# Dense tiles of eight heads in layer 0's output, work on the other batch one head pair earlier in attentions 1 and 3, and other PSUM banks in the expert stages

## The chip, the cores and the metric

The kernel runs on one core of a Trainium2 chip. The metric is device time in microseconds, the median over the runs of a kernel. The core has five engines that work beside one another, each on its own queue of instructions: TensorE (PE, with its weight loads as PEld) multiplies matrices and writes to PSUM; VectorE (DVE), ScalarE (ACT) and GpSimd (POOL) do the rest of the arithmetic; SyncE (SP) issues most DMAs. An engine that must wait for another holds up all that stands behind it in its queue. PSUM has eight banks; a bank that TensorE wrote can be written again only when its reader is done.

## The reference

Four layers act on `x` of 4 batches, 256 tokens, 256 features, in float32. Each layer adds a cross-attention to 512 context tokens of 128 features, and then a feed-forward stage. Both get `x` normalised over its features (mean and variance, no weights).

```python
x = x + L0_xattn(LN(x), ctx)        # 16 heads of 16, q and k normalised by head
x = x + L0_ffn(LN(x))               # dense W, and 4 of 64 adapters of rank 16 by norm
x = x + L1_xattn(LN(x), ctx, mask)  # 16 query heads of 128, 8 key/value heads
x = x + L1_ffn(LN(x))               # 2 of 8 experts (176 wide), and a shared one (352)
x = x + L2_xattn(LN(x), ctx, mask)
x = x + L2_ffn(LN(x))               # 1 of 2 experts by token
x = x + L3_xattn(LN(x), ctx, mask)
x = x + L3_ffn(LN(x))               # MLP on the top 12.5% of a batch's tokens
```

Layer 0's attention is the one whose output changes form. Its last 16 context tokens have key and value weights of their own and a softmax of their own:

```python
q = ln(x @ Wq + bq)                      # by head; k and k_dca likewise
ctx = attn(q, k_main, v_main) + attn(q, k_dca, v_dca)
return ctx.reshape(b, s, 16 * 16) @ Wo + bo
```

Layers 1 to 3 are `softmax(q k / sqrt(128)) v` with two query heads to a key head, then `@ Wo`.

## The kernel before, in words

The order of the instructions on TensorE, DVE, ACT and POOL is written out by hand (`manual_schedule`): what stands first in the program stands first in its engine's queue. A float32 matmul is two passes of the array, a transpose by TensorE is one.

**Layer 0.** The loop runs over batch `b`, group of four heads `hg` and half `kp` of the context; `i = 2*hg + kp` is called a half step. A half step issues: scores of this group (L1321, exponential on ACT at L1325, into `pT`); `ahead(b, i)`, which prepares the next batch; `values` of the group before (L1331 for the main context, L1340 for the last 16 tokens); at the second half `quotient`; and `between(b, i)`. The four heads of a group lie on 128 partitions of a bank `po`, 32 rows each: 16 rows that hold the softmax sum (the values have 16 columns of ones ahead of them), and 16 rows of values. `quotient` (L1354 to L1360) transposes 32 x 32 blocks on DVE to get at the sums, takes the reciprocal, transposes back, multiplies, and lets POOL add main and last part to `oT[:, hg]`. So `oT` holds four tiles of 128 partitions of which half the rows are of use. `output0` (L1366) multiplies them, for each of two chunks of 128 tokens, with `wo0`, whose four tiles are Wo's rows laid out to match (four matmuls a chunk); DVE adds the bias (`y_sb`, L1374), POOL adds to `x_sb`. The biases of the values go through the same `wo0`: `bias_columns` (`pbrow`) and `output_bias` (`pbo`, L1281). `output0(b - 1)` comes in half steps 4 and 5 of batch `b`, that of the last batch after the loop.

Keys and queries are normalised by `Scale`: POOL squares (`hs`), DVE sums (`hv`, L1218), ACT forms the roots (`hr`, L1223), DVE multiplies into `pad` (L1231), TensorE transposes (`pT`, L1296). `ahead` spreads this chain over the half steps 2 to 6.

The feed-forward stage of layer 0 works by `Arrows(n)`, one for each of eight chunks: `vectors` (`paf`, L1398), `routes` (DVE, POOL `twof`, L1414 to L1427), `turned` (transposes `puTf`, L1435), `output` (L1444, L1448).

**Attentions 1 to 3.** Query and key weights are multiplied together beforehand, as are value and output weights: `folding` has `pm` (L985, copied by ACT to `m_sb`, L993) and `pn` (L1001, copied by DVE to `n_sb`, L1004), eight pairs of them a layer, in between the work of the stage before. The attention loop has 32 units, `(b, hp)`, hp being one of eight head pairs. In a unit TensorE does the scores (`ps`, L1817), the values (`po`, L1825) and some products for queries or outputs (L1787). The sums of the softmax go over DVE and POOL: halves are added (L1836 on POOL, L1842 and L1844 on DVE), transposed and reduced to `sums` (L1850); after four head pairs TensorE multiplies them with a constant (`pz`, L1857) into the one bank "t", DVE takes the reciprocal (`rz`, L1866), spreads it (`wide`, L1871), and the outputs are multiplied by it (L1872). At the end of the attention, `last_output` (`py`, L1907) needs the last four head pairs of batch 3 divided.

After each unit the attention calls a function, `after(b, hp)`, that works on the batch before: `beside1` in attention 1 (the norm for the feed-forward stage, its transposes, the router `chosen`, L2072 to L2113, almost all DVE), `beside3` in attention 3 (norm, router's weights, `spread`, `places`; and later `gathered`, `rest`, `picked` for the batch before that).

**The banks.** In layer 0 six banks go round ("ring") and two are "o". From the second attention stage on there are four "s", two "mm", one "t" and one "o". The expert stages of layers 1 and 2 run in blocks of gathered tokens: `turn_in` (L2306 in layer 1, L2608 in layer 2) transposes a block into "t", `fall` (`pyr`, L2341, copied out by ACT at L2348) writes to "o". `pn` uses "mm", in turn with `pm`.

Of the kernel before, what the change touches and what calls it, by code (L numbers as in the profile page):

```python
# [17 lines left out]
P = 128  # L18
# [817 lines left out]
def bounded_path(ctx: ExitStack, tc: tile.TileContext, t, out: bass.AP, over):  # L836
# [137 lines left out]
    def folding(L, m_sb, n_sb):  # L974

        for i in range(4):
# [4 lines left out]
            for g in range(2):  # L981
# [18 lines left out]
                pn = bank("mm", [P, 2, D], f"pn_{L}_{i}_{g}")  # L1000
# [25 lines left out]
    with tc.manual_schedule(engines={E.PE, E.Activation, E.DVE, E.Pool}):  # L1026
# [42 lines left out]
        wo0 = l0.tile([P, 4, D], F32, tag="wo0", name="wo0")  # L1069
        nc.sync.dma_start(wo0, t["L0_wo"].rearrange("(g p) n -> p g n", p=P))  # L1070
# [34 lines left out]
        vals = [l0.tile([P, NK, H0, 32], F32, tag=f"vals{i}", name=f"vals{i}") for i in range(2)]  # L1105
        vals_d = [l0.tile([P, H0, 32], F32, tag=f"vals_d{i}", name=f"vals_d{i}") for i in range(2)]

        def ones_of_values():
# [9 lines left out]
            for i in range(2):  # L1118
                nc.gpsimd.memset(vals[i][:, : NK - 1, :, :HD0], 1.0)
                nc.gpsimd.tensor_copy(  # L1120
                    vals[i][:, NK - 1, :, :HD0], rows[:, 0:1, None].to_broadcast([P, H0, HD0])
                )
                nc.gpsimd.tensor_copy(vals_d[i][:, :, :HD0], rows[:, 1:2, None].to_broadcast([P, H0, HD0]))
# [61 lines left out]
        def project_v(b):  # L1185

            wv = by_head(wkv, 2 * HD0)[:, :, :, HD0:]
            for k0 in range(0, NK + 1, 2):
                pv = bank("mm", [P, 2, H0, HD0], f"pv{b}_{k0}")
                for k in range(k0, min(k0 + 2, NK + 1)):  # L1190
                    ck = c_last[:, b % 2, k - NK + 1, :] if k >= NK - 1 else cT[:, b, k * P : (k + 1) * P]
                    nc.tensor.matmul(pv[:, k - k0], lhsT=ck, rhs=wv[:, int(k == NK)], start=True, stop=True)
                if k0 < NK:
                    nc.scalar.copy(vals[b % 2][:, k0 : k0 + 2, :, HD0:], pv)
                else:
                    nc.scalar.copy(vals_d[b % 2][:, :, HD0:], pv[:, 0])
# [67 lines left out]
        bcol = l0.tile([P, 4, P], F32, tag="bcol", name="bcol")  # L1264

        def bias_rows():

            nc.vector.tensor_tensor(brow[:, 0, :], brow[:, 0, :], brow[:, 1, :], ALU.add)

        def bias_columns():  # L1270
            pc = bank("o", [P, 4], "pbrow")
            for g in range(4):
                nc.tensor.matmul(
                    pc[:, g : g + 1], lhsT=brow[:, 0, g * P : (g + 1) * P], rhs=ident[:1, :1], start=True, stop=True
                )
            nc.vector.tensor_copy(bcol, pc[:, :, None].to_broadcast([P, 4, P]))

        def output_bias():
            pb = bank("mm", [P, D], "pbo")
            for g in range(4):  # L1280
                nc.tensor.matmul(pb, lhsT=bcol[:, g, :], rhs=wo0[:, g, :], start=(g == 0), stop=(g == 3))  # L1281
# [45 lines left out]
        def values(b, hg, pT, po, ks, dca):  # L1327

            for k in ks:
                for j in range(4):  # L1330
                    nc.tensor.matmul(  # L1331
                        po[32 * j : 32 * (j + 1), 0, :],
                        lhsT=vals[b % 2][:, k, 4 * hg + j, :],
# [4 lines left out]
            if dca:  # L1338
                for j in range(4):
                    nc.tensor.matmul(  # L1340
                        po[32 * j : 32 * (j + 1), 1, :],
                        lhsT=vals_d[b % 2][:, 4 * hg + j, :],
# [5 lines left out]
        def quotient(b, hg, po, oT):  # L1348
# [6 lines left out]
            rz = small.tile([P, NB0], F32, tag="rz0", name=f"rz0_{b}_{hg}")  # L1355
            nc.vector.reciprocal(rz, z[:, :, 0])
            nc.vector.transpose(z, rz[:, :, None].to_broadcast([P, NB0, 32]))
            o = w0.tile([P, 2, S], F32, tag="o0", name=f"o0_{b}_{hg}")
            nc.vector.tensor_tensor(o.rearrange("p a s -> p (a s)"), po, z_f, ALU.mult)
            nc.gpsimd.tensor_tensor(oT[:, hg, :], o[:, 0], o[:, 1], ALU.add)  # L1360

        def output0(b, chunks=range(NC)):
            for c in chunks:
                py = bank("mm", [P, D], f"py0_{b}_{c}")
                for hg in range(4):
                    nc.tensor.matmul(  # L1366
                        py,
                        lhsT=oTs[b][:, hg, c * P : (c + 1) * P],
                        rhs=wo0[:, hg, :],
                        start=(hg == 0),  # L1370
                        stop=(hg == 3),
# [89 lines left out]
        xnTs[0] = layernorm_T(xn, "a0_0")  # L1461
        centred(by_head(wq0), by_head(wq0), mq)
# [51 lines left out]
        def between(b, i):  # L1514
# [25 lines left out]
            if b > 0 and i in (4, 5):  # L1540
                output0(b - 1, (i - 4,))
# [1654 lines left out]
```

## Time and profile before

| what | value |
|---|---|
| median of 3 runs | 1453.56 us (1453.41, 1453.56, 1455.87) |
| the profiled execution | 1455.58 us |
| its span | 1453.9 us |
| mean granted TensorE clock | 0.994 |
| TensorE busy | 1421.4 us |
| DVE, POOL, ACT busy | 914.0, 677.1, 585.9 us |
| layer 0's attention, feed-forward | about 20 to 146 us, 146 to 240 us |
| attentions 1, 2, 3 | about 240 to 569 us, 705 to 1000 us, 1090 to 1415 us |

The span is from the first to the last instruction of the profiled execution, and the time around it is part of the execution's own time. Busy time says how much of the span an engine worked; a row of a group gives its total busy time, the mean duration of one instruction, and the idle time ahead of it with what ended that. Matmuls overlap in the array, so that their durations are longer than the distance from one start to the next. The granted clock is given as a share of full speed: at 0.50 a matmul takes twice as long.

### The profile page before, as it was taken

What the parts mean: (1) busy time and instruction counts of PE and PEld (TensorE: products, weight loads), DVE (VectorE), ACT (ScalarE), POOL (GpSimd) and SP (SyncE); (2) the same over time, 40 slices, a digit from 0 to 9 for tenths busy, and PEclk for the clock granted to TensorE, in tenths of its full rate; (3) what the DMA queues carried; (4) which work ended last, traced back from release to release, by engine and by line L of the source; (5) the groups of instructions that cost most, each with busy time, mean ns of one, the idle gap of its engine ahead of it and who ended that gap; (6) DMA issues with size and microseconds to landing.
All of it is one profiled execution on the core that took longest, in us unless ns stands there. A gap on an engine that the chain in (4) does not pass through costs nothing.

```text
span 1453.9 us, 20222 instructions
## 1 busy us (share of the span) xinstructions
PE 1421.4 (98%) x7421; PEld 937.0 (64%) x7421; DVE 914.0 (63%) x2004; ACT 585.9 (40%) x1124; POOL 677.1 (47%) x796
## 2 busy tenths in 40 slices
PE   9999999999999999999999999999999999999998
PEld 7665676566556666777556666655875566666656
DVE  6666773666676556543576666548755766767675
ACT  4666343433433332244543333333454433333331
POOL 2222232576655454131366665665314765456560
PEclk9999999999999999999999999999999999999999
DMA  5000220310000001164020000000331000000000
GB/s 167 2 2 2 73 72 1 79 32 0 8 1 8 1 8 32 39 203 103 30 72 2 23 1 1 8 0 8 95 124 44 19 1 1 0 1 0 0 1 32
DMA packets 49591, 47.06 MB, mean 32 GB/s; under 512 B 8169, under 2 KB 45386, under 8 KB 49484
## 3 DMA queue, kind: packets, MB, share of 16 engines
q1 hardware_dynamic: 45884, 37.56, 8.6%
q0 software_dynamic: 2496, 6.82, 1.8%
q8 instruction: 61, 1.00, 0.3%
q10 hardware_dynamic: 1104, 1.31, 0.3%
q14 instruction: 46, 0.38, 0.1%
HBM read 38.86 MB, written 6.82 MB: 31 GB/s over the span
## 4 chain that ended last, share of the span: by engine, by line
PE 88%; DVE 7%; POOL 2%; issue 1%; ACT 1%; DVEq 0%; ACTq 0%; POOLq 0%
PE ps L1817 22%; PE po L1825 21%; PE paq L1787 5%; PE pao L1787 4%; PE pbq L1787 4%; PE pbo L1787 4%; PE pgu L2325 2%; PE ps L1321 2%; PE pyf L1448 2%; PE po L1331 2%; PE paf L1398 1%; PE py L1907 1%; PE pm L985 1%; PE psh L2161 1%; PE pn L1001 1%
## 5 line engine op out<-in xcount | busy, mean ns | idle before, releaser
L1836 POOL TENSOR_TENSOR half<-pT 128x1024 f32<-128x1024 f32 x93 | 218.8, 2353 | 322.6 <-ACT pT L1820 255.2
L1817 PE MATMUL ps<-qT,cT 128*128 128x512 f32 x768 | 345.5, 592 | 0.0
L1825 PE MATMUL po<-pT,c_sb 128*128 128x512 f32 x768 | 345.3, 592 | 0.0
L1820 ACT ACTIVATE pT<-ps,mbias 128x512 f32<-128x512 f32 x384 | 263.7, 687 | 155.5 <-PE ps L1817 143.9
L1825 PEld LDWEIGHTS po<-pT,c_sb 128*128 128x128 f32 x768 | 145.8, 190 | 183.2 <-issue 183.2
L1817 PEld LDWEIGHTS ps<-qT,cT 128*128 128x128 f32 x768 | 138.9, 190 | 138.4 <-issue 137.0
L1829 ACT COPY oT<-po 128x512 f32<-128x512 f32 x96 | 56.2, 586 | 265.0 <-PE po L1825 265.0
L1872 POOL TENSOR_TENSOR oT<-oT,wide 128x512 f32<-128x512 f32 x90 | 115.5, 1304 | 27.9 <-DVE wide L1871 27.9
L1325 ACT ACTIVATE pT<-ps 128x512 f32<-128x512 f32 x128 | 66.1, 603 | 37.8 <-PE ps L1321 37.6
L1797 DVE TENSOR_TENSOR qT<-qT,paq 128x128 f32<-128x128 f32 x90 | 25.5, 283 | 85.8 <-ACT qT L1796 85.7
L1797 DVE TENSOR_TENSOR w<-w,pao 128x128 f32<-128x128 f32 x21 | 6.0, 285 | 109.4 <-ACT w L1796 109.4
L1844 DVE TENSOR_TENSOR half<-half 128x512 f32<-128x512 f32 x96 | 71.0, 740 | 2.5 <-POOL half L1836 2.2
L1846 DVE STREAM_TRANSPOSE turned<-half 128x512 f32<-128x512 f32 x96 | 68.3, 712 | 6.3
L1787 PEld LDWEIGHTS paq<-xnT_a,m_sb 128*128 128x128 f32 x360 | 57.9, 191 | 21.5 <-issue 10.6
L1787 PE MATMUL paq<-xnT_a,m_sb 128*128 128x128 f32 x360 | 71.4, 280 | 0.1
L1787 PE MATMUL paq<-xx,m_x 128*128 128x128 f32 x360 | 69.8, 276 | 0.0
L1850 DVE TENSOR_REDUCE sums<-turned 128x16 f32<-128x512 f32 x96 | 65.9, 686 | 3.4
L1787 PE MATMUL pao<-n_x,ox 128*128 128x128 f32 x336 | 65.4, 276 | 0.3 <-POOL ox L1713 0.3
L1871 DVE STREAM_TRANSPOSE wide<-rz 128x512 f32<-128x512 f32 x96 | 62.2, 686 | 0.1
L1796 ACT COPY qT<-paq 128x128 f32<-128x128 f32 x90 | 23.9, 265 | 89.9 <-PE paq L1787 89.8
L1800 DVE TENSOR_TENSOR qT<-qT,pbq 128x384 f32<-128x384 f32 x90 | 49.9, 554 | 9.4
L1787 PEld LDWEIGHTS paq<-xx,m_x 128*128 128x128 f32 x360 | 54.6, 192 | 0.0
(445 smaller groups left out, 2612.9 us busy)
## 6 DMA issues: line engine op xcount, KB each, us to landing
wo<-in_L_wo SPq DMA_DIRECT2D x12, 512.0 KB
wq<-in_L_wqT SPq DMA_DIRECT2D x11, 512.0 KB
yd<-yr SPq DMA_DIRECT2D x23, 128.0 KB
w<-in_F_w SPq DMA_DIRECT2D x4, 512.0 KB
xd<-xn_f SPq DMA_DIRECT2D x7, 256.0 KB
wk<-in_L_wkT SPq DMA_DIRECT2D x11, 128.0 KB
wv<-in_L_wvT SPq DMA_DIRECT2D x11, 128.0 KB
x_sb<-in_x SPq DMA_DIRECT2D x4, 256.0 KB
```

Of the source, the lines that this page charges most:

```text
L1325: nc.scalar.activation(pT[kp][:, j], ps[j], AF.Exp)
L1787: nc.tensor.matmul(p[:, at, :], lhsT=lhsT, rhs=rhs, start=(k == 0 and at == 0), stop=(k == len(of) - 1 and i == which[-1]),)
L1817: nc.tensor.matmul(ps, lhsT=cT[:, b, k * P : (k + 1) * P], rhs=qT, start=True, stop=True)
L1820: nc.scalar.activation(pT[:, k, :], ps, AF.Exp, bias=mbias[:, b, k : k + 1])
L1825: nc.tensor.matmul(po, lhsT=c_sb[:, b, k, :], rhs=pT[:, k], start=(k == 0), stop=(k == NK - 1))
L1829: done["head"] = nc.scalar.copy(raw, po).ins
L1836: nc.gpsimd.tensor_tensor(half, pT[:, 0:2], pT[:, 2:4], ALU.add)
L1844: nc.vector.tensor_tensor(part, half[:, 0], half[:, 1], ALU.add)
L1846: nc.vector.transpose(turned.rearrange("p f i -> p (f i)"), part)
L1850: nc.vector.tensor_reduce(sums[b, hp // 4][:, hp % 4, :], turned, AX.X, ALU.add)
L1871: nc.vector.transpose(wide, rzs[b, hp // 4][:, hp % 4, :, None].to_broadcast([P, NB, 32]))
L1872: eng.tensor_tensor(outs[b, hp], outs[b, hp], wide.rearrange("p f i -> p (f i)"), ALU.mult)
```

## The change

There are four groups of edits.

1. Layer 0's output. Groups `hg` 0 and 1 share one tile of `oT`, and 2 and 3 the other: even groups have their values in rows 16 to 31 of each 32 and odd ones in rows 0 to 15. `vals` and `vals_d` are laid out accordingly, so the value weights are copied once into the new order by POOL (`wvo`), the values' copies by ACT go in two halves, and the ones are filled in halves. `quotient` writes the reciprocal into one of two columns of a persistent, zeroed `rz0`, so that the rows of the other group are multiplied by zero, and POOL adds an odd group's two parts to what the even group left. `wo0` has two tiles, read by eight DMAs of 16 partitions. `output0`, `pbrow` and `pbo` use two matmuls in place of four. `output0(b - 1)` comes in half steps 6 and 7 in place of 4 and 5, for batches 1 and 2 (in the last batch it stays at 4 and 5). After the loop, `arrows[0].turned()` and `output()` come ahead of the last batch's output.
2. `beside1`: everything one head pair earlier (hp 3 to 6 in place of 4 to 7).
3. `beside3`: the same, and `gathered`, `rest` one head pair later (hp 1 and 2 in place of 0 and 1), `picked` with `rest`.
4. Banks: `turn_in` of both expert stages takes "t" and "o" in turn, `fall` takes "mm", and `pn`, once the ring is gone, takes "o".

```diff
-                pn = bank("mm", [P, 2, D], f"pn_{L}_{i}_{g}")
+                pn = bank("mm" if "ring" in banks else "o", [P, 2, D], f"pn_{L}_{i}_{g}")
...
-        wo0 = l0.tile([P, 4, D], F32, tag="wo0", name="wo0")
-        nc.sync.dma_start(wo0, t["L0_wo"].rearrange("(g p) n -> p g n", p=P))
+        wo0 = l0.tile([P, 2, D], F32, tag="wo0", name="wo0")
+        wo0r = t["L0_wo"].rearrange("(q o j i x) n -> o j i x q n", q=2, o=2, j=4, i=2)
+        for o in range(2):
+            for j in range(4):
+                r0 = 32 * j + HD0 * (1 - o)
+                nc.sync.dma_start(wo0[r0 : r0 + HD0], wo0r[o, j, 1])
...
+        halves = [(slice(HD0, 32), slice(0, HD0)), (slice(0, HD0), slice(HD0, 32))]
+
+        rz0 = [l0.tile([P, 2 * S // 32, 2], F32, tag=f"rzh{i}", name=f"rzh{i}") for i in range(2)]
+        wvo = l0.tile([P, 2, 2, H0 // 2, HD0], F32, tag="wvo", name="wvo")
...
-                if k0 < NK:
-                    nc.scalar.copy(vals[b % 2][:, k0 : k0 + 2, :, HD0:], pv)
-                else:
-                    nc.scalar.copy(vals_d[b % 2][:, :, HD0:], pv[:, 0])
+                for o, (h, _) in enumerate(halves):
+                    if k0 < NK:
+                        nc.scalar.copy(vals[b % 2][:, k0 : k0 + 2, o, :, h], pv[:, :, o])
+                    else:
+                        nc.scalar.copy(vals_d[b % 2][:, o, :, h], pv[:, 0, o])
...
             pb = bank("mm", [P, D], "pbo")
-            for g in range(4):
-                nc.tensor.matmul(pb, lhsT=bcol[:, g, :], rhs=wo0[:, g, :], start=(g == 0), stop=(g == 3))
+            for g in range(2):
+                nc.tensor.matmul(pb, lhsT=bcol[:, g, :], rhs=wo0[:, g, :], start=(g == 0), stop=(g == 1))
...
-            rz = small.tile([P, NB0], F32, tag="rz0", name=f"rz0_{b}_{hg}")
-            nc.vector.reciprocal(rz, z[:, :, 0])
-            nc.vector.transpose(z, rz[:, :, None].to_broadcast([P, NB0, 32]))
+            odd = hg % 2
+            rz = rz0[odd]
+            nc.vector.reciprocal(rz[:, :, 1 - odd], z[:, :, HD0 * odd])
+            nc.vector.transpose(
+                z.rearrange("p f (i x) -> p f i x", i=2), rz[:, :, :, None].to_broadcast([P, NB0, 2, HD0])
+            )
             o = w0.tile([P, 2, S], F32, tag="o0", name=f"o0_{b}_{hg}")
             nc.vector.tensor_tensor(o.rearrange("p a s -> p (a s)"), po, z_f, ALU.mult)
-            nc.gpsimd.tensor_tensor(oT[:, hg, :], o[:, 0], o[:, 1], ALU.add)
+
+            oT = oT[:, hg // 2, :]
+            nc.gpsimd.tensor_tensor(oT, oT if odd else o[:, 1], o[:, 0], ALU.add)
+            if odd:
+                nc.gpsimd.tensor_tensor(oT, oT, o[:, 1], ALU.add)
...
-                for hg in range(4):
+                for q in range(2):
                     nc.tensor.matmul(
                         py,
-                        lhsT=oTs[b][:, hg, c * P : (c + 1) * P],
-                        rhs=wo0[:, hg, :],
-                        start=(hg == 0),
-                        stop=(hg == 3),
+                        lhsT=oTs[b][:, q, c * P : (c + 1) * P],
+                        rhs=wo0[:, q, :],
+                        start=(q == 0),
+                        stop=(q == 1),
                     )
...
+        for n in range(2):
+            wv = by_head(wkv, 2 * HD0)[:, n, :, HD0:].rearrange("p (q o j) x -> p o q j x", q=2, o=2)
+            for o in range(2):
+                nc.gpsimd.tensor_copy(wvo[:, n, o].rearrange("p (q j) x -> p q j x", q=2), wv[:, o])
...
-            if b > 0 and i in (4, 5):
-                output0(b - 1, (i - 4,))
+
+            i0 = 4 if b == B - 1 else 6
+            if b > 0 and i in (i0, i0 + 1):
+                output0(b - 1, (i - i0,))
...
         arrows[1].routes()
+        arrows[0].turned()
+        arrows[0].output()
         output0(B - 1)
...
-            arrows[n].turned()
+            if n:
+                arrows[n].turned()
...
-                arrows[n].output()
+                if n:
+                    arrows[n].output()
...
-            if hp == 4:
+            if hp == 3:
                 ahead1[b] = Norm(b - 1, f"f1_{b - 1}")
+            elif hp == 4:
+                ahead1[b] = ahead1[b].tokens()
             elif hp == 5:
-                ahead1[b] = ahead1[b].tokens()
+                turned1(b - 1, ahead1[b])
             elif hp == 6:
-                turned1(b - 1, ahead1[b])
-            elif hp == 7:
                 chosen(b - 1)
...
-                    pt = bank("t", [P, ND, P], f"pxg{self.j}")
+                    pt = bank("to"[self.j % 2], [P, ND, P], f"pxg{self.j}")
...
-                    py = bank("o", [P, D], f"pyr{j}")
+                    py = bank("mm", [P, D], f"pyr{j}")
...
-            pt = bank("t", [P, ND, P], f"pxg2_{self.j}")
+            pt = bank("to"[self.j % 2], [P, ND, P], f"pxg2_{self.j}")
...
-            if hp == 4:
+            if hp == 3:
                 routers[b - 1] = Router(b - 1)
-            elif hp == 5:
+            elif hp == 4:
                 routers[b - 1].tokens()
                 routers[b - 1].weights()
+            elif hp == 5:
+                routers[b - 1].spread()
             elif hp == 6:
-                routers[b - 1].spread()
-            elif hp == 7:
                 routers[b - 1].places()
         if b > 1:
-            if hp == 0:
+            if hp == 1:
                 routers[b - 2].gathered()
-            elif hp == 1:
+            elif hp == 2:
                 routers[b - 2].rest()
-            elif hp == 2 and b == 3:
-                picked(0)
+                if b == 3:
+                    picked(0)
```

## The prediction

> **What bounds the kernel now.** I read the page first, then the table of stretches, then TensorE's waits, then single stretches.
>
> ```profile
> span 1453.9 us, 20222 instructions
> ...
> PE 1421.4 (98%) x7421; PEld 937.0 (64%) x7421; DVE 914.0 (63%) x2004; ACT 585.9 (40%) x1124; POOL 677.1 (47%) x796
> ...
> PE 88%; DVE 7%; POOL 2%; issue 1%; ACT 1%; DVEq 0%; ACTq 0%; POOLq 0%
> ```
>
> TensorE works 1421.4 of 1453.9 us and carries 88% of the chain of waits. Only two things can help: fewer passes of the array, or a part of the 32.5 us in which it idles. Where these lie, the stretches show (columns: time, its length, busy time of PE, PEld, DVE, ACT, POOL, granted clock, DMA share, GB/s):
>
> ```profile
> 20.00:146.00 126.00, 120.51 (x1345) 78.72 (x1344) 82.75 (x166) 81.72 (x158) 30.34 (x42) 1.00 0.04 11
> 146.00:240.00 94.00, 90.48 (x463) 64.47 (x462) 63.30 (x116) 39.16 (x90) 29.41 (x27) 1.00 0.18 57
> 240.00:557.00 317.00, 315.45 (x1351) 191.83 (x1351) 194.34 (x418) 122.57 (x211) 181.49 (x216) 1.00 0.06 16
> 557.00:705.00 148.00, 140.58 (x807) 111.19 (x806) 71.94 (x220) 54.55 (x155) 36.14 (x41) 0.97 0.33 96
> 705.00:1000.00 295.00, 293.81 (x1249) 178.86 (x1248) 182.01 (x403) 111.05 (x188) 172.27 (x196) 0.99 0.05 16
> 1000.00:1100.00 100.00, 96.92 (x522) 75.57 (x521) 67.38 (x150) 46.72 (x95) 35.90 (x41) 1.00 0.26 80
> 1100.00:1408.00 308.00, 307.03 (x1325) 186.86 (x1324) 212.72 (x431) 114.56 (x194) 178.49 (x204) 1.00 0.03 8
> 1408.00:1454.00 46.00, 38.11 (x266) 32.87 (x264) 26.91 (x74) 7.97 (x19) 7.42 (x11) 0.95 0.07 25
> ```
>
> The bodies of attentions 1 to 3 (rows 3, 5, 7) leave 1.6, 1.2 and 1.0 us: nothing is to be had inside them. Layer 0 leaves 5.5 us, its FFN 3.5, the stretch behind attention 1 leaves 7.4. TensorE's waits name the places:
>
> ```profile
> PE pz L1857 <- DVE sums L1850: 3.4, 3, 2.6
> PE pxg L2608 <- ACT xnT_f L940: 1.7, 1, 1.7
> PE py L1366 <- POOL oT L1360: 1.6, 1, 1.6
> PE pT L1296 <- DVE y_sb L1374: 1.4, 1, 1.4
> PE pysh L2178 <- ACT m_sb L993: 0.6, 1, 0.6
> PE pxg L2961 <- DVE rz L1866: 0.6, 2, 0.3
> ```
>
> **Layer 0.** Removed: in the output 2 of 4 matmuls for each of 8 chunks.
>
> ```profile
> L1366 PE MATMUL py<-wo,oT 128*128 128x256 f32 x64 | 15.8, 390 | 1.6 <-POOL oT L1360 1.6
> ```
>
> 64 records are 32 matmuls of two passes. A pass of 256 columns takes 0.215 us from start to start in undisturbed rows (0.39 in the row is latency), so 32 passes are 6.9 us; 4 passes of pbo are 0.9 more, and 2 of 4 one-column pbrow matmuls 0.3. So 8.1 us of TensorE is taken out, 1.72 for each batch's output. It comes through only where the array is the bound. By batch:
> - Batch 0: only pbo and pbrow shrink. TensorE waits twice here for the chain DVE sums, ACT square root, DVE pad (1.4 us at 47.2, 1.0 at 51.5), which does not shorten. The copies of the values to their halves, 3 on ACT (512 wide 0.58, 256 wide 0.38), become 6, about 0.25 us more, ahead of that chain's ACT part. I put the start at 0.
> - Batch 1: output0(0) leaves half steps 4 and 5 for 6 and 7. Then py no longer covers the pad chain: hv 71.73 to 73.72 on DVE, hr on ACT till 75.25 (behind four exponentials), pad product at 77.27 to 79.03. The transposes pT at 81.00 would now start about 3.4 us of PE work earlier, and wait for that chain, which gains about 0.5. In return the 1.42 us wait of pT at 83.07 for y_sb (the copy out of a bank, queued on DVE behind the next Norm) goes, and the outputs come back later at half price. I count 1.72 + 1.58 less about 1.4 of new waits for pad and y_sb: 1.9.
> - Batch 2: the same without the 1.58: 1.72 less a wait for pad of about 0.6: 1.1.
> - Batch 3: its outputs stay at 4 and 5, 1.7. A wait of 1.3 at 130.4 (pxn behind a quotient on DVE) stays.
> - The start of the FFN: TensorE waited 1.75 from start to start (1.6 in the row) for POOL's oT at 163.30, because POOL was busy with twof from 160.21 to 162.14. Now the set that needs twof (turned(0), output(0)) stands ahead of py. It must wait for 162.14, about 1.9 in the same place; the wait of py lies behind it. Gain 1.72 + 1.75 - 1.9 = 1.6. arrows[0] leaves its later place; DVE's routes(2) comes about 1.2 us later, and is needed at 182: free.
>
> Added at nothing: POOL's four wvo copies (a 128x256 copy is 0.42 in its rows) at 8 to 10 us, before the values need them; twelve smaller fills for six, about 0.8 us more, ending some 3 us before the first use at 32.6; the second add (0.74) of each odd head group, 8 in all, on a POOL that is busy 30 of 126 us. Only the last of these is near the path, and it is inside the 1.9.
>
> wo0 is read by 8 DMAs of 16 partitions, 32 KB each, in place of one of 512 KB. Rows: SP took 0.43 us to issue wo at 10.13, so seven more add 3 us, ahead of bo, wa, wb, ww and the bias; wo itself and bo are first used at 40.5 and 44, the others from 146 on. The Trainium skill speaks against this: "DMA: Bandwidth & Descriptors", Rules for kernel authors, wants many small transfers coalesced, since under 64 KB one pays mostly overhead. By the trace's issue row it is 3 us on SP hidden by 25 us; by the rule, with eight overheads laid one behind the other at the roughly 2 us that the page gives as fixed cost of its GpSimd path, an estimate of 16 us from 10, still before 40. I take 0. Sum for layer 0: **6.3** (bounds 3.5, if the chains of batches 1 and 2 eat all, and 9).
>
> **Attention 1, work moved up one head pair.** At hp 4 to 7 an undisturbed head pair lasts 8.43 us, all TensorE. The sums on DVE are ready 3.2 us before pz needs them at hp 3; with the Norm there, slack falls to 1.2 to 1.85, as in attention 2, whose Norm is at hp 3 already. No wait, so 0 in the body. At the end chosen(2) sits on DVE (558.61 to 561.87) ahead of the last sums:
>
> ```profile
> 562.00:565.60 3.60, 0.96 (x9) 0.80 (x8) 2.80 (x6) 0.27 (x1) 0.00 (x0) 1.00 0.01 2
> 565.60:569.00 3.40, 3.40 (x18) 3.40 (x17) 3.33 (x5) 0.00 (x0) 1.27 (x1) 0.50 0.00 0
> ```
>
> pz starts at 564.88, 2.8 us late. Without chosen the sums are there at about 560.9, and pz starts at 562.07. Behind it pbo takes 2.7 us, now at full clock, then py must wait for the division chain (rz, wide on DVE, oT on POOL: pz + 4.0 for its first tile, + 5.9 for its last): a new wait of 1.2. py starts at 566.1 in place of 569.49: 3.4, less 0.2 for its last tile: **3.2** (bounds 1.4, the chain being longer than read; 4.5, wait and half clock both gone).
>
> The clock: in this trace the array was busy 0.96 of 3.6 us, and the next 3.4 us ran at 0.50, at a price of 1.7. A stall of 1.75 at 163.30 left it at 1.00. The Trainium skill, "TensorE: Matmul & The Clock Gate", The HAM clock gate, gives half rate after an idle window of about 3.4 us, in windows that run free. By its word a partly busy window costs nothing; by the row it costs 1.7. The row decides; the 1.2 that is left is nearer the 1.75 that cost none. Half clock also stands at 599.8 to 606.6 and 777.3 to 780.7. As everything before them moves by about 9 us, windows may fall otherwise: 1.7 each way on each.
>
> **Banks in the expert stages.** Block loop of layer 1: 2.76 us a block, TensorE bound, nothing; its last fall waits 0.7 for yr (one bank): 0.7. Second turn_in at 613: pgu waits for DVE's we at 614.3 anyway: 0. pysh at 684.3, behind an ACT copy: 0.8. Layer 2: second turn_in 0.6; pxg of block 5 at 1048.7, bank held by xnT_f: 1.8. Against it, pn gets one bank, and each pn must await the copy of the one before:
>
> ```profile
> 696.22 1.12 PE L1001 MATMUL pn<-wo,wv 128*128 128x512 f32 x2 [0.69 <-ACT m_sb L993]
> 696.38 0.80 DVE L925 TENSOR_SCALAR xn_a<-x_sb,mv_a,rstd_a 128x256 f32<-128x256 f32 x2 [0.84 <-POOL rstd_a L920]
> 697.10 1.28 DVE L1004 COPY n_sb<-pn 128x512 f32<-128x512 f32 x2
> ```
>
> The copy lasts 0.69 and the pm between two pn 0.9, so mostly it is free. Here DVE is held by the Norm's wait for POOL: two copies end at 697.8 and 698.4, so the pn of 696.22 waits till 697.8, 1.6, of which about 0.6 is the wait of the pm behind it: -1.0. The same in layer 3's fold (1086.32 against a copy that ends at 1087.43): -1.1. Sum 0.7 + 0.8 + 0.6 + 1.8 - 2.1 = **1.8** (bounds -1 and 4).
>
> **Attention 3.** pxg waits behind pz's bank for rz twice, 0.53 from start to start at 1260.9 and 1344.6; a head pair later rz is not in the way: 1.1. The last pz, 0.64 late behind places: 0.5. Sum **1.6** (0.5 to 1.7).
>
> Sum 6.3 + 3.2 + 1.8 + 1.6 = 12.9. The profiled execution lasted 1455.58 (1.7 outside its span), 2.0 above the median of 1453.56; its span would go to 1441.0. From the median: **1440.7**.
>
> **Rivals.**
> 1. Layer 0 isn't TensorE's any more: with py at half price the pad chain sets batches 1 and 2, and the FFN start waits for twof as long as before for oT. For it: DVE 82.8 and ACT 81.7 of 126 us, and the waits at 47 and 51. Layer 0 then gives 3.5 and pn's bank takes 1 us more: 12.9 - 2.8 - 1 = 9.1, so 1444.5, and with a half-clock window more 1446.2. Chance 0.22.
> 2. More comes: attention 1's tail gives 4.5, layer 0 7.5, and one half-clock window falls away: 1.3 + 1.2 + 1.7 more, 1436.5. For it: the waits exist, and the windows hang on phase. Chance 0.14.
> 3. Slower: pn's single bank. If DVE stands 1.3 us late at each of the 14 follow-on folds of layers 2 and 3, as at 696, that is 14 x 1.3 = 18 us against 2.1 counted: 1456.6. It decides from a copy that ends more than 0.2 us after the pm between. Against it: in the other twelve follow-on folds the trace has the copy end before the next pn starts, though five times only by 0.05 to 0.1. Chance 0.04.
> 4. The change does not do what it says: moved Norms push pz late where they land, so that waits only change place and gain stays under 2.9: slack 1.2 speaks against it. Chance 0.03, 1452.
>
> Mine: 0.57. The range of 8 in 10 takes my case with clock windows of 1.7 each way and most of 1 and 2: 1435.5 to 1446.5. About 0.2% (2.9 us) is what a measurement can tell from no change here: faster 0.93, same 0.03, slower 0.04.
>
> **What would show it.** Right: 32 records of L1366's matmul; the pz wait of 2.6 gone, and one of about 1.2 at the last py; the L2608 and pysh waits gone; new waits of pn for n_sb near 690 and 1080; new waits of pT for pad in layer 0. Wrong: layer 0 shorter by under 4 or over 8 us, waits of pz in hp 4 of attentions 1 or 3, or half clock in other windows than before.

## The result, and the profile after

The changed kernel takes 1443.36 us (median; 1440.92 to 1444.77), the kernel before 1453.63 in the same comparison: ratio 0.9924, interval 0.9907 to 0.9941, a gain of 8.6 to 13.5 us where 12.9 was forecast. A second comparison gave 0.9923 (0.9909 to 0.9937). The spans of the two profiled executions differ by 10.9 us.

The page and the stretches of the changed kernel come first. The stretches are cut at the same work as those shown of before (columns as there).

```profile
span 1443.0 us, 20195 instructions
...
PE 1413.3 (98%) x7381; PEld 931.5 (65%) x7381; DVE 895.7 (62%) x2005; ACT 585.8 (41%) x1136; POOL 684.1 (47%) x816
```

```profile
20.00:143.80 123.80, 118.23 (x1310) 75.17 (x1309) 80.60 (x163) 81.18 (x166) 35.48 (x56) 0.97 0.05 15
143.80:236.40 92.60, 88.91 (x455) 63.02 (x455) 64.23 (x120) 39.04 (x90) 30.88 (x30) 1.00 0.18 57
236.40:553.40 317.00, 315.45 (x1357) 192.52 (x1356) 191.65 (x437) 122.76 (x212) 180.70 (x217) 1.00 0.06 16
553.40:698.80 145.40, 139.63 (x801) 111.08 (x800) 71.08 (x202) 54.37 (x154) 36.09 (x40) 0.96 0.34 98
698.80:992.20 293.40, 292.05 (x1249) 177.37 (x1248) 181.88 (x403) 111.05 (x188) 172.36 (x196) 1.00 0.05 16
992.20:1091.50 99.30, 96.70 (x522) 76.36 (x521) 67.58 (x150) 46.52 (x95) 35.96 (x41) 1.00 0.26 80
1091.50:1397.80 306.30, 306.05 (x1330) 187.12 (x1329) 199.32 (x434) 114.39 (x194) 178.88 (x206) 1.00 0.03 8
1397.80:1443.00 45.20, 37.79 (x261) 32.33 (x259) 25.76 (x71) 8.22 (x20) 7.06 (x10) 0.98 0.07 26
```

Lengths against before: layer 0's attention 126 to 123.8, its feed-forward stage 94 to 92.6, attention 1 the same to 557, then 148 to 145.4, attention 2 295 to 293.4, layer 2's stage 100 to 99.3, attention 3 308 to 306.3, the end 46 to 45.2. Two things stand out. Layer 0's clock fell from 1.00 to 0.97, and attention 2, which nothing in the change touches, is 1.6 shorter, with a clock of 1.00 for 0.99.

TensorE's waits:

```profile
PE pn L1001 <- DVE n_sb L1004: 4.4, 3, 2.3
PE puTf L1461 <- POOL twof L1453: 3.0, 2, 1.8
PE pT L1315 <- DVE pad L1244: 2.7, 3, 1.5
...
PE py L1943 <- POOL oT L1908: 0.9, 3, 0.5
...
PE pz L1893 <- DVE sums L1886: 0.3, 1, 0.3
```

The old waits (pz 2.6, pxg of layer 2, pysh, py for oT, pT for y_sb, pxg for rz) are gone. New are the waits of pn for the copy of the pn before, of pT for pad, and most of puTf's for twof (3.0 in two waits, where before had one of 1.3). The output's matmuls are half as many:

```profile
L1392 PE MATMUL py<-wo,oT 128*128 128x256 f32 x32 | 8.7, 399 | 0.0
```

Matching the starts of the same work in both profiles gives each part's share. "Profile" is how much earlier the work behind the part starts than in the profile of before, less what was gained ahead of it.

| part | forecast | profile | part alone or undone, by ratio of runs |
|---|---|---|---|
| layer 0 with its feed-forward stage | 6.3 | 3.65 | 7.1 (5.2 to 9.2) alone |
| tail of attention 1 | 3.2 | 3.2 | 3.6 (2.5 to 4.8) alone |
| turn_in, fall, and pysh | 3.9 | 3.9 | 2.6 (1.5 to 3.6) alone, pysh not in it |
| pn on one bank | -2.1 | -3.9 | about -3.1, undone, with pysh's wait back |
| attention 2 (clock) | 0 | 1.6 | |
| attention 3 | 1.6 | 2.6 | 3.2 (1.7 to 4.5) alone |

The profile's column adds up to 11.0 before rounding. In layer 0's row 0.6 is no gain: the first scores start that much earlier in this span than in before's, and in other spans up to 0.9 later. The runs' column adds up to 13.4, with intervals of a microsecond or two on each row, because an execution may hold one 1.7 us clock window more or less than the next.

### The profile page after: what moved, and what is told of

It reads as the page before. It is cut to its first block, busy times and chain, and to the rows that moved or that the text cites. A ratio compares the mean times of both kernels' runs of the same rounds, so it can differ in the third digit from the quotient of the medians.

```text
span 1443.0 us, 20195 instructions
## 1 busy us (share of the span) xinstructions
PE 1413.3 (98%) x7381; PEld 931.5 (65%) x7381; DVE 895.7 (62%) x2005; ACT 585.8 (41%) x1136; POOL 684.1 (47%) x816
## 5 line engine op out<-in xcount | busy, mean ns | idle before, releaser
L1836 DVE TENSOR_TENSOR qT<-qT,pbq 128x384 f32<-128x384 f32 x90 | 49.9, 554 | 10.1 <-PE ps L1853 0.9
```

## The experiments

Gains in microseconds are worked out from the ratio and the kernel before of the same comparison (1455.3, 1455.3 and 1455.0 us).

### The changed kernel again

No edit.

> The changed kernel once more, for a second profile and more runs. In its first profile layer 0 up to the end of its feed-forward stage was 3.65 us shorter than before (forecast 6.3), and the clock was at 0.50 from 28.3 to 31.7 and from 48.8 to 52.2. Theory 1: those windows are chance of phase, as the array idles 1.5 us there before as after; this profile has them elsewhere or not at all, and without them layer 0 is 6 to 7 us shorter than before. Theory 2: the change brings them (a wait of 1.8 for pad at 47.9 in place of 1.45), so they stand there again and layer 0 gains 3.6 again. Both: median 1442 to 1444.

Measured: 1444.88, ratio 0.9923 (0.9909 to 0.9937). The granted clock in the first profile of the changed kernel, with the window ahead of each slow one:

```profile
24.90:28.30 3.40, 2.97 (x31) 1.86 (x27) 1.75 (x6) 2.89 (x6) 3.40 (x15) 1.00 0.07 16
28.30:31.70 3.40, 3.40 (x9) 2.22 (x8) 0.00 (x0) 1.62 (x4) 0.48 (x3) 0.50 0.00 0
45.30:48.70 3.40, 1.92 (x23) 1.55 (x23) 3.23 (x7) 3.01 (x7) 0.00 (x0) 1.00 0.00 0
48.70:52.10 3.40, 3.40 (x27) 1.80 (x29) 3.26 (x8) 1.41 (x2) 1.64 (x3) 0.51 0.00 0
```

And the second profile of the same kernel:

```profile
28.90:32.30 3.40, 3.40 (x13) 2.33 (x14) 0.52 (x1) 1.34 (x3) 0.22 (x1) 0.50 0.00 0
48.70:52.10 3.40, 3.07 (x42) 1.89 (x39) 3.22 (x9) 1.87 (x3) 1.45 (x2) 1.00 0.00 0
131.30:134.70 3.40, 3.40 (x32) 1.50 (x32) 0.37 (x1) 2.06 (x4) 0.68 (x1) 0.50 0.00 0
```

The window at 28 stands again, the one at 49 does not, and one at 131 has come. So a window is not bound to the code: which waits are followed by half clock differs between executions of one kernel. Theory 1's stronger half did not show: layer 0 was again two windows poorer, and only 2.4 shorter than before (counted from the first scores, 2.1 here and 3.1 in the first profile).

### pn on its two banks

```diff
-                pn = bank("mm" if "ring" in banks else "o", [P, 2, D], f"pn_{L}_{i}_{g}")
+                pn = bank("mm", [P, 2, D], f"pn_{L}_{i}_{g}")
```

> The changed kernel with pn back in the two banks mm. Theory 1: pn's single bank costs a wait and a half-clock window at the Norm of each fold: the waits of 2.5 at 689 and 2.0 at 1077 go back to the 1.5 and 0.85 of before, the stretch from the last turn_in of layer 1 to attention 2 is 2.5 shorter, the fold before attention 3 1.5 shorter: together 3 to 4 us below the changed kernel, 1439.5 to 1440.5. Theory 2: the Norm's own wait on DVE for POOL sets when attention starts, and the bank only shows it: under 1 us, 1442.5 to 1443.4.

Measured: 1441.74, ratio 0.9901 (0.9886 to 0.9916), against 0.9923 with pn on "o" on the same chip: 3.1 us better, as theory 1 has it and three times what theory 2 allows, though the two intervals overlap a little. What the single bank does is read in the changed kernel, PE first and then DVE (start, duration, instruction, idle before):

```profile
689.11 1.13 PE L1001 MATMUL pn<-wo,wv 128*128 128x512 f32 x2 [2.30 <-DVE n_sb L1004]
```

```profile
687.65 0.80 DVE L925 TENSOR_SCALAR xn_a<-x_sb,mv_a,rstd_a 128x256 f32<-128x256 f32 x2 [0.85 <-POOL rstd_a L920]
688.37 0.68 DVE L1004 COPY n_sb<-pn 128x512 f32<-128x512 f32 x1
```

The copy is queued on DVE behind the Norm, the Norm waits 0.85 for POOL, and pn starts when the copy ends at 689.05. That is the wait that was forecast (2.47 from start to start in place of 0.86 and 0.65: -1.0). What was not in the sum came behind it:

```profile
687.10:690.50 3.40, 1.40 (x6) 0.92 (x7) 1.63 (x4) 1.25 (x5) 2.60 (x4) 0.99 0.14 39
690.50:693.90 3.40, 3.40 (x12) 2.26 (x11) 0.99 (x2) 1.51 (x5) 1.77 (x2) 0.50 0.39 116
```

TensorE stood 2.0 of 3.4 us, and the next 3.4 us ran at half clock, in both profiles of the changed kernel (690.5 and 691.1). With pn on "mm" there is no half clock between 601 and 1436.

But the wait does not always bring the window. Three kernels further down (`fill0` under "Work in layer 0's waits", `dense_out45` under "The outputs at half steps 4 and 5", `arrows_later` under "The first adapters behind the last output") also have pn on "o", with the same wait of 2.2 to 2.3 at this fold, and none has half clock behind it. `fill0`:

```profile
686.80:690.20 3.40, 1.57 (x8) 1.09 (x9) 1.80 (x4) 1.07 (x5) 2.60 (x4) 1.00 0.13 39
690.20:693.60 3.40, 3.40 (x20) 2.41 (x20) 0.97 (x2) 2.58 (x7) 1.60 (x2) 1.00 0.40 116
```

By matched starts this fold costs 0.9 in these three profiles and 2.4 to 2.5 in the two with the window. The second one, at 1077, costs 1.4 to 1.7 in four profiles, and 2.5 in `fill0`, where half clock follows at 1075.9. So the single bank costs 2.3 to 2.6 by itself, and 1.0 to 1.5 more in an execution that has one of these windows. Putting pn back also brings back a wait of pysh (further down), so that the 3.1 of the runs is what is left after that.

### Layer 0 alone

The kernel before with all edits to layer 0 and no other.

> The kernel before with the layer 0 edits alone (dense tiles, outputs in half steps 6 and 7, arrows[0] first). Forecast was a gain of 6.3. Theory 1 (half-clock windows of chance hid part of it): 5 to 6.5 us below before, 1447 to 1448.6, and in the profile no new wait of more than 1 us except the one for pad at 48. Theory 2 (the pad chain and the start eat it): 3 to 4 us below, 1449.6 to 1450.6.

Measured: 1448.28, ratio 0.9951 (0.9937 to 0.9964): 7.1 us. Theory 2's 3 to 4 is outside, theory 1's 5 to 6.5 inside. Its profiled execution was the slowest of its runs (1449.75 of 1447.52 to 1449.75) and has half clock at 28.3 and at 48.8; its layer 0 looks, like the changed kernel's first, only 3.6 shorter.

Nor is the kernel before free of windows in layer 0. The profile of the kernel that has its layer 0 unchanged, and attention 1's edit alone, shows them behind the wait of 1.3 for xn:

```profile
130.40:133.80 3.40, 2.34 (x32) 1.44 (x36) 2.60 (x8) 1.88 (x4) 1.45 (x2) 1.00 0.01 2
133.80:137.20 3.40, 3.40 (x36) 1.83 (x28) 1.37 (x3) 1.73 (x4) 0.08 (x1) 0.50 0.00 0
137.20:140.60 3.40, 3.40 (x27) 1.49 (x20) 2.06 (x4) 2.07 (x4) 0.74 (x1) 0.50 0.02 5
```

All three profiles with the old layer 0 besides that of before have them there. That one had none, and carried a window at 777 instead. Counted from the first scores to the feed-forward stage's second set of chunks, the old layer 0 takes 1.6, 3.2 and 3.2 us longer in those three than in the profile of before. The five profiles with the new layer 0 and nothing else in it (the changed kernel twice, this one, `pn_mm` with pn on its two banks, and `pn_first_o` below) take 2.1 to 4.9 less than it, 3.6 in the mean. The two means lie 5.6 apart. So one pair of profiles undersells this part, and 5.6 is inside the runs' interval, below the 6.3 that was forecast.

### Work in layer 0's waits

```diff
                 pt = bank("t", [P, 4, P], f"pT{b}_{c}")
+                for _ in range(6 if (b, c) == (1, 0) else 0):
+                    nc.tensor.matmul(pt[:, 0, :], lhsT=ident, rhs=ident, start=True, stop=True)
...
         pt = bank("t", [P, ND, S], f"pxn_{name}")
+        for _ in range(2 if name == "a0_1" else 0):
+            nc.tensor.matmul(pt[:, 0, :P], lhsT=ident, rhs=ident, start=True, stop=True)
```

> The changed kernel with eight extra 128x128 matmuls on TensorE: two ahead of the transposes of batch 1's norm (a wait of 0.4 at 26.0), six ahead of the first transposes of batch 1's pad (a wait of 1.8 at 47.9); they write banks that the transposes then overwrite, and stand in waits. Theory 1 (the array's idleness in these waits brings the half-clock windows at 28.3 and 48.8): no half clock from 24 to 56, 1.5 to 3 us below the changed kernel, 1440.4 to 1442. Theory 2 (windows come from elsewhere, or don't come in most runs): within 0.7 us of the changed kernel.

Measured: 1443.25, ratio 0.9916 (0.9903 to 0.993), against 1444.88 and 0.9923: better by 1.0 (ratio) or 1.6 (medians), inside the noise of both. The profile is clear:

```profile
24.00:56.00 32.00, 30.81 (x344) 21.15 (x346) 22.12 (x51) 21.14 (x40) 10.36 (x23) 1.00 0.05 14
```

Full clock through batch 0, and none of the windows of layer 0 was slow. That is no accident of one profile: all seven profiles with the new layer 0 and no extra products have a half-clock window between 28 and 53 us, and the three with them (this one, `best` and `best_plist` below) have none. In this profile layer 0's parts can be read without the clock: from the first scores (24.5 in before) to the feed-forward stage's second set it is 5.1 shorter than before, batch 0 at 0.0 (forecast 0).

### The outputs at half steps 4 and 5

```diff
-            i0 = 4 if b == B - 1 else 6
-            if b > 0 and i in (i0, i0 + 1):
-                output0(b - 1, (i - i0,))
+            if b > 0 and i in (4, 5):
+                output0(b - 1, (i - 4,))
```

> The changed kernel with output0(b-1) in half steps 4 and 5 for every batch, as before; the tiles stay dense. In the changed kernel's profiles batches 1 and 2 gained 1.3 and 1.2 us, where the output's passes alone are 1.7 each: the rest went into new waits for pad (0.9 twice), and for qT and y_sb. Theory 1: at 4 and 5 the output covers the pad chain again, the waits for pad go, and each batch gains its 1.7, so 0.5 to 1 us below the changed kernel: 1442.4 to 1444.4 on the chip of the last runs (where it had 1444.9). Theory 2: the move was what the saving needed, since pT waits for y_sb behind the Norm on DVE (1.6 at 83 before): 1 to 2.5 us above the changed kernel.

Measured: 1446.97, ratio 0.9945 (0.9932 to 0.9959): 3.2 us above the changed kernel by ratio, 2.1 by median. Theory 2. The wait that was 1.4 in before:

```profile
PE pT L1315 <- DVE y_sb L1400: 3.6, 2, 2.3
```

With the output's passes halved and left in place, TensorE reaches pT earlier and waits 2.3 in batch 1 and about 1.3 in batch 2 (no such wait in before) for a copy (y_sb) that sits on DVE behind the Norm. Half clock follows from 84.4 to 91.2. So half of the 1.7 that is taken out of batch 1 at 4 and 5, and three quarters of batch 2's, is waited for at once: batch 2, which the half clock does not reach, gains 0.6 in place of the changed kernel's 1.2. Moving the outputs behind the pad chain costs waits of 0.9 for pad, and takes these away. How the 2.1 to 3.2 us divide between the waits and the half clock was not measured, and the interval overlaps that of the changed kernel a little.

### The first adapters behind the last output

The two edits that move `arrows[0].turned()` and `output()` are undone.

> The changed kernel with arrows[0].turned() and output() back in their place behind the last output. Theory 1: the last py then waits for POOL's oT, now two adds of 0.74 behind twof, about 2.5 us; of the 1.4 that the start of the feed-forward stage gained only 0.1 is left: 1.0 to 1.5 us above the changed kernel. Theory 2: the wait for twof took the place of the wait for oT, one for one, and the order is worth nothing: within 0.4.

Measured: 1446.14, ratio 0.9935 (0.9921 to 0.9949): 1.3 (median) to 1.7 us above the changed kernel. The intervals overlap, but the profiles settle it for theory 1: the start of the feed-forward stage gains 1.4 over before in the changed kernel and 0.0 here. The wait, against 1.8 for twof in the changed kernel:

```profile
PE py L1392 <- POOL oT L1386: 3.3, 1, 3.3
```

POOL makes twof first, and then the two adds of an odd group. In the changed order the wait for twof covers them, and the last py waits for nothing.

### Attention 3 alone

> The kernel before with the edits to beside3 alone. Forecast 1.6; in the two profiles of the changed kernel the stretch from 1170 to 1421 is 2.5 shorter. Theory 1: 2.5, of which 1.1 are the waits behind pz's bank, 0.6 the last pz, and the rest weight loads or copies that no longer stand beside the scores' products, in every run. Theory 2: 1.6, and the remaining 0.9 comes with another edit (the phase of other parts): 1.4 to 1.8 us below before.

Measured: 1452.07, ratio 0.9978 (0.9969 to 0.9988): 3.2 us, theory 1; 1.4 to 1.8 is at the interval's edge. The part that the forecast lacked shows in before, not among TensorE's waits but among those of its weight loads:

```profile
PEld paq L1787 <- DVE xnT_a L1721: 0.2, 1, 0.2
```

At 1236.5 and 1320.5 the query products start 0.42 late in all (start to start), as DVE is late with the folded input of the next queries. One head pair later this DVE work meets other neighbours, and most of the 0.42 is gone, twice. 2 x (0.53 + 0.42) + 0.6 is 2.5; the part is 2.6 shorter in this kernel's own profile as in the changed kernel's.

### turn_in and fall alone

> The kernel before with turn_in on t and o in turn, and fall on mm; pn stays in mm. Forecast 3.9 for these (0.7, 0.8, 0.6, 1.8). Theory 1: these waits are all on the path: 3.5 to 4.3 us below before, nothing new behind them. Theory 2: what is gained in the blocks is waited for again at the gathers of the Norm behind them (POOL): under 2.5 us.

Measured: 1452.60, ratio 0.9982 (0.9975 to 0.999): 2.6 us, between the two theories. The waits of 0.6 and 1.8 in layer 2 and 0.7 at the last fall are gone, 3.1 in all, of which matched starts show 2.7 as gained (2.0 and 0.6 before rounding); but the one of pysh, 0.8 in my sum, stays:

```profile
PE pysh L2178 <- ACT m_sb L993: 0.6, 1, 0.6
```

So that 0.8 was put to the wrong edit. It is pn that frees it (the same wait is there in `pn_mm`, and not in the changed kernel, whose work behind it gains 1.1): pysh takes an "mm" bank that a fold's first pm holds until ACT's copy, and finds the other one free if pn is elsewhere.

### Attention 1 alone

> The kernel before with the edits to beside1 alone. Forecast 3.2, and in both profiles of the changed kernel the stretch from 558 to 576 is 3.3 shorter. Theory 1: 2.8 to 3.8 us below before, pz no longer waits, and py waits about 0.4 and 0.7 for the divided outputs. Theory 2 (the shift only trades one clock window for another, as those behind plist at 600): under 1.5.

Measured: 1451.75, ratio 0.9975 (0.9967 to 0.9983): 3.6 us, theory 1. The window that holds the end of attention 1 in the changed kernel, to be set against 0.96 of 3.6 busy and then 0.50 before:

```profile
558.90:562.30 3.40, 3.14 (x27) 2.90 (x26) 3.30 (x6) 0.00 (x0) 1.27 (x1) 1.00 0.00 0
```

The tail is 3.2 shorter by matched starts in this kernel's own profile too. In the changed kernel pz no longer waits; py waits 0.43 and 0.68 from start to start for the divided outputs, 1.1 in all, where 1.2 was forecast.

### pn on "o" for a layer's first two folds, and more work in waits

```diff
-                pn = bank("mm" if "ring" in banks else "o", [P, 2, D], f"pn_{L}_{i}_{g}")
+                pn = bank("o" if i == 0 and "ring" not in banks else "mm", [P, 2, D], f"pn_{L}_{i}_{g}")
```

> The changed kernel with pn on o only for the first two of each layer's eight folds, and on mm for the rest. In the profile of banks_turn_fall (pn on mm throughout) the wait of pysh of 0.8 behind the ACT copy of pm stays; in the changed kernel it is gone. Theory 1: that 0.8 belongs to pn, since pn on o leaves pysh the other mm bank; here both are had: 0.5 to 1 us below pn_mm, 3.6 to 4.2 below the changed kernel. Theory 2: the wait moves to the next pm or pn: equal to pn_mm within 0.4.

Measured: 1440.08, ratio 0.9901 (0.9886 to 0.9916): 3.2 us better than the changed kernel, and the same ratio as pn_mm, as theory 2 has it. But the wait of pysh is gone from the profile and comes nowhere else: by matched starts the work behind it gains 1.1 here and 0.1 in pn_mm. So theory 1's mechanism holds, and its size is below what these runs can tell.

`best` adds to it the extra matmuls of above, and five ahead of batch 3's first feed-forward transposes; `best_plist` adds also:

```diff
+                    if n == 0:
+                        state["fill"] = bank("o", [P, P], "pfill")
+                    for _ in range(5 if n == 0 else n % 2):
+                        nc.tensor.matmul(state["fill"], lhsT=ident, rhs=ident, start=True, stop=True)
                     nc.tensor.matmul(
                         state["plist"], lhsT=at, rhs=state["bring"][:, i, c], start=(n == 0), stop=(n == 2 * N8 - 1)
                     )
```

> pn_first_o with extra 128x128 matmuls in three waits of layer 0: two ahead of the norm's transposes of batch 1, six ahead of batch 1's first pad transposes, five ahead of batch 3's first transposes for the feed-forward stage. Theory 1 (an idle array in these waits brings half-clock windows at about 28, 47 to 49 or 131 in most executions): 1.4 to 2.5 us below pn_first_o, no half clock before 560 in the profile. Theory 2 (no effect on the clock in most executions): within 0.7.

> best with extra matmuls at plist (layer 1's lists, at about 590): five ahead of its first, and one behind every second of its 32 small ones, into a free bank. In all profiles so far half clock stands for 6.8 us behind these small matmuls. Theory 1: TensorE's low activity there brings it, and the extra matmuls keep full clock; the window's part that falls on psh and pysh (1.7 of the 3.4) is saved: 1 to 2 us below best, unless 32 more passes lengthen plist. Theory 2: plist is as long as DVE makes it, the extra work only comes on top: 0 to 2 us above best.

Measured: `best` 1439.69, ratio 0.9899 (0.9884 to 0.9914): no gain over pn_first_o that the runs show, theory 2, though its profile has no half clock before 590. `best_plist` 1437.92, ratio 0.9882 (0.9867 to 0.9897), 1.8 below `best` by median. The intervals overlap, but each of its four runs lies below all four of `best`, and from plist to the next gather its profile is 1.7 shorter by matched starts: theory 1. (The forecast miscounted: plist is 16 products of 46 columns in 32 passes, and 13 products were added, 26 passes.) The stretch around plist, `best` and then `best_plist`:

```profile
578.00:600.00 22.00, 20.84 (x99) 18.06 (x99) 15.16 (x68) 2.96 (x6) 3.93 (x4) 0.84 0.06 17
```

```profile
578.00:600.00 22.00, 21.95 (x133) 19.62 (x132) 15.66 (x69) 3.48 (x8) 3.83 (x4) 1.00 0.06 17
```

More work, and the clock stays full. `best_plist` has no half clock in its profile until 1433.8 (mean 0.999), and its runs lie within 1.2 us of each other (1437.24 to 1438.41), where the changed kernel's lie within 3.9. It is the fastest kernel of the study, 17 us below before and about 6 below the changed kernel.

## Why the prediction was right or wrong, point by point

- *The whole.* The time and its sign came as forecast; 12.9 was 1.9 to 2.6 too much by the three ways of counting (ratio, medians, spans). That it came so near is partly luck: at full clock layer 0 fell 1.2 short of its forecast and attention 3 exceeded its own by 1.0. Two of the signs named for being wrong did show in the first profile, layer 0 shorter by under 4 us and half clock in other windows than before. The next points say why.
- *Layer 0, 6.3.* The runs of the part alone give 7.1 (5.2 to 9.2). The steps are read best where no clock window disturbs, in `fill0` against before: batch 0 0.0 (forecast 0), batch 1 1.3 (1.9), batch 2 1.2 (1.1), batch 3 1.2 (1.7), the start of the feed-forward stage 1.4 (1.6), 5.1 in all. Batch 1 was mis-sized: beside the wait for pad (0.9) a second one of 0.8 for qT came in the next half step. Batch 3 has a new wait of about 0.4 for the second norm. That moving the output is part of the saving was in the working, and the experiment that left it at 4 and 5 agrees.
- *Where the profile and the runs part.* Of the 2.65 us that the first profile lacks in layer 0, 2.05 lie in batch 0, which holds both half-clock windows and takes that much longer than in before; at full clock, in `fill0`, it takes the same. The rest is the 1.2 above, less the 0.6 by which this span's scores start earlier. The profiled execution was the slowest of its kernel's runs.
- *Attention 1, 3.2.* Right in size and in its parts: pz's wait gone, a wait of 1.1 behind it, full clock.
- *Banks, 1.8.* The sum came out at 0.0 in the profile. The gains were 3.9 as forecast, though pysh's came by way of pn. Of pn's costs, the first fold's wait was 0.9 where 1.0 was worked out, and the second's 1.4 to 1.7 where it was 1.1. The term that was missing is the half-clock window of 1.5 us that follows the wait of 2.3 at 689 in both profiles of the changed kernel, though in none of the other three with this wait. The prediction had set 1.7 either way for clock windows in the range, but did not ask which of its own new waits was long enough to bring one, though it had the row for it: 0.96 of 3.6 us busy, then 0.50.
- *Attention 3, 1.6.* The mechanism held; 0.42 twice was missing, since I read TensorE's waits but not those of its weight loads.
- *Attention 2, 0.* The 1.6 there is a half-clock window of before's profile (777 to 781) that no other profile of the study shows near that place, save one (at 770). It is no effect of an edit.
- *Rivals.* Rival 1's two halves split: layer 0 did not fall to 3.5 (5.1 at full clock), and pn's bank took 0.2 to 0.5 us more than forecast by itself, 1 to 2 us more with a window. Rival 2's 4.5 for attention 1 did not come. Rival 3's bank waits at the two Norms, 2.3 and 1.9 us, and not at all folds. Rival 4 did not come: pz's waits are 0.3 in all.
- *The weighings.* For the clock, the row rather than the idle window of the Trainium skill's page "TensorE: Matmul & The Clock Gate" decided. It was right that a partly busy window can cost: windows that were busy for 1.40, 1.92 and even 2.97 of 3.4 us were followed by half clock. But the row was no rule either, since the one of `fill0` that was busy for 1.57 was not. That these windows run free, as that page says in its section on the HAM clock gate, fits the traces: within each profile the half-clock stretches start whole multiples of 3.413 us apart, and one wait falls differently on that grid from execution to execution. The eight small DMAs cost nothing that shows: they were issued from 10.1 to 14.6, landed 4.4 us later in the median, and were first used at 41.1.

What stays open: what share of activity decides the clock. The busy time of the rows does not, as two windows of before show. Ahead of 599.8, where the clock halves, TensorE was busy nearly throughout, with plist's products of 46 columns; behind the second, half busy, the clock stays full:

```profile
596.40:599.80 3.40, 3.36 (x27) 3.02 (x26) 3.40 (x16) 0.00 (x0) 0.00 (x0) 0.99 0.00 0
1046.90:1050.30 3.40, 1.75 (x16) 1.59 (x15) 1.09 (x2) 2.13 (x4) 0.00 (x0) 1.00 0.91 272
1050.30:1053.70 3.40, 3.40 (x25) 3.14 (x24) 1.96 (x3) 1.94 (x3) 0.00 (x0) 1.00 1.06 349
```

A wait of 1.9 at 160 (start to start), behind 512-wide products, was never followed by half clock; one of 0.4 at 26 between scores of 16 rows was, in both profiles of the changed kernel and in that of layer 0 alone. That narrow products count for less was argued from this and from plist, not measured by itself.

## What to carry to other kernels

When work is taken off the bounding engine, ask of each place what that work covered: here the halved output was worth its passes only where it was moved behind the chain that it had hidden. A bank that is shared to free another brings a wait whose size is the queue ahead of the copy that empties it, at its worst place. A wait of some two microseconds on TensorE can bring a half-clock window on top, here at the first fold in two of five profiles with the same wait, so it belongs in the range rather than in the sum. Before a profile's stretches are set against each other, list the half-clock windows of both: here they took 2.0 us from the gain of layer 0 and added 1.6 to that of attention 2, which the change does not touch.

## What the runs showed that I had not expected

- A wait of TensorE can be filled with extra matmuls at no cost in place: six 128x128 products in a wait of 1.8 left batch 0 where it was, and kept its clock at 1.00. What that is worth in the kernel's time, the runs do not tell.
- The 16 small products of plist (32 passes in 5.7 us at 589, paced by DVE) go with half clock in all of the other 13 profiles, for 3.4 to 10.2 us; at 0.50 the passes start 0.213 us apart in place of 0.112. 13 extra products among them took 1.8 us off the median of `best`.
- The spread of a kernel's runs is largely the clock. In the largest comparison the kernel before ran 25 times, from 1453.1 to 1457.1 us: the three runs with a mean granted clock of 0.996 took 1453.2 on average, the seven with 0.995 1454.1, the fourteen with 0.994 1455.8.
